# Order of users of two PSUM banks, stacked taps, a copy by DMA and a gate on other engines in a four-layer convolution and attention kernel

## The chip, the cores and the metric

The kernel runs on one core of one Trainium2 chip. The metric is the device time of one execution in microseconds. All times are of that core; a profile is one execution recorded by the hardware profiler.

## What is computed

The input x has 4 samples of 256 channels on a 48 x 48 grid (2304 positions), float32 throughout. Four layers follow, each added to x after a group norm of x over 32 groups:

```
x = x + attention(gn(x))     # layer 0: 8 heads of 64; q and k normed over positions
x = x + gated(gn(x))         # layer 1: gate from pooled, blurred, depthwise-filtered x
x = x + nonlocal(gn(x))      # layer 2: one head of 64; output normed over the batch
x = x + refine(gn(x))        # layer 3: channel gate, depthwise 3x3, instance norm, leaky

# layer 0, per sample
q, k, v = split(w_qkv @ x)
q, k = l2norm(q), l2norm(k)                  # along the 2304 positions
out = w_out @ (softmax(10 * q.T @ k) @ v) + b_out

# layer 1
t = blur_pool(max_pool_3x3(x), stride=3)     # 16 x 16
s = conv_h1(t) + conv_v1(t) + skewed_h2(t) + skewed_v2(t)   # depthwise 11x3 and 3x11
gate = sigmoid(bn(s));  out = x * upsample(gate)

# layer 2
theta, phi, g = theta_w @ x, phi_w @ x, g_w @ x              # 64 channels each
y = softmax(theta.T @ phi / 8) @ g.T;  out = batchnorm(W_w @ y)

# layer 3
a = sigmoid(w2 @ leaky(w1 @ mean(x)));  y = depthwise_3x3(x * a) + b
out = leaky((y - mean(y)) / sqrt(var(y) + eps))
```

The four depthwise filters of layer 1 add up to one filter of 81 distinct taps per channel.

## The kernel before

**Units and groups.** Attention works on units: 384 queries of one pair of heads (layer 0: 4 samples x 4 pairs x 6 = 96 units) or of one sample (layer 2: 4 x 3 = 12 units, two halves of the queries in the two halves of the partitions). A unit has 18 key blocks of 128, taken two at a time: nine groups a unit. A group issues its scores (`scores`, L322, quarter-array products of 64x64, and the exponential L328 on ScalarE), and after that the weighted sums of the group before (`weigh`, L342). Row sums are taken by adding the exponentials up on VectorE (`add_up`, L362 and L368), with halves on GpSimd for some groups (L353). There are eight buffers of exponentials, two for a group.

**Tables by group.** `attend` walks over the groups. Everything else is hung on a group: `fills` and `due` map a group's number to jobs; a job of `fills` has a rank, and the jobs of one group run in the order of their ranks, between the scores and the weighted sums. The order of issue on every engine is the order of the program. In layer 0, group 2 of each unit (`AT_CHUNK`) carries a chunk of the next pair's projection: q (rank 1), v (2), the square sum of q (2.2), k (4.5), its eviction, square sum and the next load (4.7). It also carries the output projection of the unit before (`out_proj`; first half at 2.5, or 0 in sample 0; second at 4), the row sums of that unit (`total`, 4.6), a group norm's column products (`of_means`, `of_squares`, 4.65, read at 4.8) and, in a pair's last chunk, the bias of the values two pairs on (`norms`, after all of them). After some ranks (`EVICTED`) one of layer 1's products on ScalarE (`take_taps`) is let in.

**Banks.** All these products go through two PSUM buffers, `pj`, each one bank, handed out in turn. A tile's users, on whatever engine, keep the order of the program. `of_k` lets the row sums and the norm's products use spare columns of k's bank. So one chunk uses: q first bank, v second, output 0 first, output 1 second, k first, with sums and norm columns behind k. In sample 0 the first output comes ahead of q.

**Row sums.** `total` multiplies the sums into rows, ScalarE copies them (`row`, L386), SP's queue sends them to a partition-wise layout (L388), `invert` takes the reciprocal on VectorE two groups later (L392), SP's queue sends it back and spreads it (L396, L401), and `divide` (L419) multiplies it in on GpSimd nine groups after the unit's end.

**Layer 1.** The first three samples run under layer 0: pooling on VectorE (`maxima`), products of taps on ScalarE (L899), sums on VectorE (L922). The last sample runs under layer 2 as four lanes (`l1_last`), generators that take one step a group, except in a unit's first group: the norm, `tops` (pooling of both channel halves), `sums` and `gates` (gate, statistics, and the norm for layer 2). `sums` runs `strips_pe` for one channel half after the other: 81 taps in seven rounds of twelve, each tap a diagonal 64x64 matrix (`build`, L950, on GpSimd) times a window of the padded map `pd` (L966), four quarter-array products abreast, in two banks; ScalarE copies four quarter results (L974) and VectorE adds them (L981, L984). Groups in `taken` carry other work for `pj`, and no round is issued there.

**Layer 2's projection.** `project2` computes for each slice of 384 positions phi and theta in one product (`both`, L1081) and g in another (`g`, L1102). ScalarE copies phi into both halves of the keys `kd` (L1087), and theta into `qv` (L1092). Sample 0's slices lie in the last pair's chunks of layer 0, those of samples 1 and 2 two at a time in layer 2's groups, those of sample 3 in `follow`, which waits for the norm, takes three steps, and lays out what is left in the last group of sample 2.

**Layer 3.** Tiles of one sample and channel half go through the conv (L1753) in six steps of 24 products. Each step's events run by rank. `put_before` brings the next tile: product (L1530), addition onto x (`grow`, L1592), squares; pads are shifted into four row groups by DMA and by engines (L1630 to L1636). A `Chain` for each sample turns square sums into the channel gate, in steps placed by `GATE_AT`; its matrix products write into spare columns of the conv's bank (`g_tile`) and VectorE reads them there (L1683, L1701).

Of the kernel before, what the change touches and what calls it, by code (L numbers as in the profile page):

```python
# [17 lines left out]
NK = 2  # L18
# [60 lines left out]
def usual_path(  # L79
# [40 lines left out]
    nc.gpsimd.memset(mhalf, -0.5)  # L120
    vec = cpool.tile([P, 9, NK], F32, name="vec")
# [65 lines left out]
    of_k, clock = {}, {"t": -1}  # L187
# [12 lines left out]
    def gn(b, res, halves=range(NK), slices=range(NSL), first=False, placed=False):  # L200
# [62 lines left out]
        if placed:  # L263

            t = clock["t"] + 1
            t += (AT_AFTER - t) % NG
            fills.setdefault(t, []).extend([(4.65, of_means), (4.8, squares)])
            fills.setdefault(t + NG, []).extend([(4.65, of_squares), (4.8, inverse)])
            due.setdefault(t + NG + 3, []).append(done)
            yield 1  # L270
            return
# [100 lines left out]
    def total(u):  # L372

        if of_k.get("t") == clock["t"]:
            ps = of_k["ps"][:, 392 : 392 + QC]
        else:
            ps = pj_tile()[:, :QC]
# [78 lines left out]
    EVICTED = (1, 2, 4, 4.7)  # L456
# [3 lines left out]
    def last(u, t):  # L460
# [12 lines left out]
        else:  # L473
            at_total = AT_TOTAL if "shift" in u["of"] else AT_CHUNK
            todo = [
                (fills, at_total, (4.6, lambda: total(u))), (due, AT_FOLD, lambda: fold(u, nc.gpsimd)),
# [79 lines left out]
    def project(b, norm, pair):  # L556
# [17 lines left out]

        def norms():

            w = at["w"]
            ps = pj_tile()
            for k in range(NK):
                nc.tensor.matmul(  # L580
                    ps[:, 0:1], lhsT=w[:, k, 2, :], rhs=norm["nb"][:, k : k + 1],
                    start=k == 0, stop=k == NK - 1,
                )
            pair["bias_v"] = small.tile([P, 1], F32, tag="bias_v", name="bias_v", bufs=3)
            nc.vector.tensor_copy(pair["bias_v"], ps[:, 0:1])
# [72 lines left out]
        def chunk(s):  # L658
# [7 lines left out]
            def end():  # L666
                at["evict"]()
                square(s, 1)
                if s + 2 < NCH:
                    fetch(s + 2)  # L670

            return [
                (1, query), (2, lambda: values(s)), (2.2, lambda: square(s, 0)), (4.5, key),
                (4.7, end),
# [10 lines left out]
        def rescale(c0, c1):  # L685
# [10 lines left out]
            "prefetch": prefetch, "norms": norms, "start": start,  # L696
# [6 lines left out]
    def out_proj(b, p, c, pair, o):  # L703

        cols = slice(c * SL, (c + 1) * SL)

        def part(k):
            ps = pj_tile()
# [4 lines left out]
            )  # L713
            if c == 0:
# [12 lines left out]
        return [((2.5 if b else 0, 4)[k], lambda k=k: part(k)) for k in range(NK)]  # L727
# [23 lines left out]

    def tap_weights():
# [6 lines left out]
        nc.gpsimd.tensor_add(ident2, ident[:, 0:D], ident[:, D:P])  # L759
        yield 2  # L760
# [21 lines left out]
        while i < len(TAPS):  # L782
# [6 lines left out]
            yield 1  # L789
        v1 = lp.tile([P, NK], F32, name="v1")  # L790
# [6 lines left out]
    WEIGHT_TICKS = 26  # L797

    NT = 4
# [3 lines left out]
    L1_BUF = (NT + 1) * AS * AS  # L803
# [123 lines left out]
    TAPS_AT_ONCE = 12  # L927

    AT_PLACE = 7

    def strips_pe(b, k, norm, res):


        rounds = [
            range(i, min(i + TAPS_AT_ONCE, len(TAPS)))
            for i in range(0, len(TAPS), TAPS_AT_ONCE)
        ]
        diag = {}
        acc = lp.tile([P, AS, AS], F32, tag=("l1acc", "blur2")[k], name="l1acc")
        res["acc"] = acc  # L940
        parts = wo.rearrange("p c n -> p (c n)").rearrange(
            "p (i h r c) -> p i h r c", i=2, h=2, c=AS
        )

        def build(n):
            taps = rounds[n]
            xs = xsp.tile([P, NK, SL + 1], F32, tag="xs", name="diag1")
            xs = xs.rearrange("p k s -> p (k s)")[:, : len(taps) * D]
            diag[n] = xs.rearrange("p (t j) -> p t j", j=D)
            nc.gpsimd.tensor_tensor(  # L950
                diag[n], ident2.unsqueeze(1).to_broadcast([P, len(taps), D]),
                wt[:, k, taps[0] : taps[-1] + 1].unsqueeze(2).to_broadcast([P, len(taps), D]),
                ALU.mult,
            )

        def product(n):
            taps = rounds[n]
            ps = [pj_tile()[:, : AS * AS] for _ in HALVES]
            runs = [taps[0::2], taps[1::2]]
            for i in range(len(runs[0])):  # L960
                for h, r in enumerate(HALVES):
                    for e, run in enumerate(runs):
                        if i >= len(run):
                            continue
                        dr, dc = TAPS[run[i]]
                        nc.tensor.matmul(  # L966
                            ps[h][HALVES[h ^ e]].rearrange("p (r c) -> p r c", c=AS),
                            lhsT=diag[n][r, run[i] - taps[0], :],
                            rhs=pd[r, PAD + dr : PAD + dr + AS, PAD + dc : PAD + dc + AS],
                            start=i == 0, stop=i == len(run) - 1,  # L970
                        )
            for h, r in enumerate(HALVES):
                for e in range(2):
                    nc.scalar.copy(  # L974
                        parts[r, n % 2, e].rearrange("p r c -> p (r c)"), ps[h][HALVES[h ^ e]]
                    )

        def add(n):
            two = parts[:, n % 2]
            if n == 0:  # L980
                nc.vector.tensor_add(acc, two[:, 0], two[:, 1])  # L981
                return
            for e in range(2):
                nc.vector.tensor_add(acc, acc, two[:, e])  # L984
# [3 lines left out]
        while "blurred" not in res or "nb" not in norm:  # L988
            yield 1
        pd = padded(k, norm, res)  # L990
# [1909 lines left out]
```

## Time and profile before

| | us |
|---|---|
| median of 3 runs | 3505.92 |
| lowest, highest | 3504.39, 3508.83 |
| profiled execution, its own time | 3503.65 |
| its span | 3501.90 |
| PE busy | 3430.2 (98%) |
| VectorE busy | 2541.1 (73%) |
| ScalarE busy | 2331.2 (67%) |
| GpSimd busy | 793.9 (23%) |

How to read it: "busy" is the time in which an engine had an instruction at work; matmuls are pipelined, their ends are modelled, and a wait shorter than the pipeline is not seen in "busy", only in the distance between starts. Layer 0 runs from the start to about 2896 us, layer 2 (with layer 1 of the last sample) to about 3341, layer 3 to the end. The profile's lines that carry the argument stand in the prediction.

### The profile page before, as it was taken

How to read it: one execution, taken by the hardware profiler on the slowest of the kernel's cores; microseconds unless marked ns; L12 is line 12 of the kernel's file. 1: busy time of each engine (PE TensorE's matmuls, PEld its weight loads, DVE VectorE, ACT ScalarE, POOL GpSimd, SP SyncE). 2: the span in 40 equal slices, each digit the busy share in tenths (PEclk: the TensorE clock that was granted, in tenths of full speed). 3: DMA queues.
4: the chain of work that ended last, by engine and by line, in shares of the span. 5: the costliest groups of instructions: out<-in, count | busy, mean ns of one | idle time of the engine just before them, and what ended most of it. 6: DMA issues, size and time to landing. Idle time of an engine off the chain costs nothing.

```text
span 3501.9 us, 89386 instructions
## 1 busy us (share of the span) xinstructions
PE 3430.2 (98%) x37990; PEld 1728.2 (49%) x37990; DVE 2541.1 (73%) x3352; ACT 2331.2 (67%) x3751; POOL 793.9 (23%) x668
## 2 busy tenths in 40 slices
PE   9999999999999999999999999999999999999988
PEld 5454545454444444444444444444444444554533
DVE  3455545467788788687887886868887879757677
ACT  5555655555885686557866875568658855555577
POOL 2333333320101010001110100001010106667432
PEclk9999999999999999999999999999999999999999
DMA  2211111111111111121111111111111110000057
GB/s 90 49 27 22 26 22 22 27 22 27 22 32 22 26 22 26 43 58 22 27 17 26 22 26 22 27 12 32 16 30 13 31 13 6 6 6 8 4 144 234
DMA packets 102759, 116.33 MB, mean 33 GB/s; under 512 B 39712, under 2 KB 93840, under 8 KB 101584
## 3 DMA queue, kind: packets, MB, share of 16 engines
q1 hardware_dynamic: 101104, 108.63, 16.4%
q8 instruction: 300, 4.92, 0.6%
q10 hardware_dynamic: 1248, 1.91, 0.2%
q14 instruction: 107, 0.88, 0.1%
HBM read 56.99 MB, written 11.80 MB: 20 GB/s over the span
## 4 chain that ended last, share of the span: by engine, by line
PE 86%; DVE 9%; issue 2%; ACT 1%; POOL 1%; DMA 1%; DVEq 0%; SPq 0%; POOLq 0%; ACTq 0%
PE av L342 33%; PE sc L322 33%; PE pj L615 8%; PE pj L710 3%; PE pj L649 3%; DVE acc L368 3%; PE cv L1753 2%; PE pj L381 1%; PE pj L966 1%; PE pj L1081 1%; DVE x L1029 1%; ACT kd L1087 0%; DVE x L1848 0%; DVE x L723 0%; DMA sh<-pad 0%
## 5 line engine op out<-in xcount | busy, mean ns | idle before, releaser
L328 ACT ACTIVATE pt<-sc 128x768 f32<-128x768 f32 x1944 | 1473.4, 810 | 696.8 <-PE sc L322 692.6
L368 DVE TENSOR_TENSOR acc<-acc,pt 128x768 f32<-128x768 f32 x1368 | 1362.8, 996 | 209.6 <-ACT pt L328 114.3
L342 PE MATMUL av<-pt,v 64*64 64x384 f32 x13824 | 1274.7, 484 | 0.0
L322 PE MATMUL sc<-q,k 64*64 64x384 f32 x13824 | 1269.9, 482 | 0.5 <-ACT pt L328 0.5
L322 PEld LDWEIGHTS sc<-q,k 64*64 64x64 f32 x13824 | 525.5, 133 | 589.4 <-issue 558.5
L342 PEld LDWEIGHTS av<-pt,v 64*64 64x64 f32 x13824 | 518.2, 133 | 564.4 <-issue 521.6
L419 POOL TENSOR_TENSOR o<-o,rinv 128x384 f32<-128x384 f32 x95 | 117.4, 1236 | 1702.5 <-DMA rinv<-rinv 1691.4
L353 POOL TENSOR_TENSOR half<-pt 128x768 f32<-128x768 f32 x189 | 365.8, 1939 | 508.9 <-ACT pt L328 438.5
L368 DVE TENSOR_TENSOR acc<-acc,half 128x768 f32<-128x768 f32 x171 | 187.1, 1094 | 223.3 <-POOL half L353 222.5
L899 ACT ACTIVATE prod<-pd,wt 128x256 f32<-128x256 f32 x486 | 340.7, 761 | 0.2
L723 DVE SCALAR_TENSOR_TENSOR x<-pj,bo,x 128x384 f32<-128x384 f32 x192 | 118.1, 617 | 256.0 <-PE pj L710 254.7
L615 PE MATMUL pj<-xs,w 128*128 128x384 f32 (+1 forms) x720 | 277.5, 508 | 3.9 <-DVE x L723 3.9
L615 PEld LDWEIGHTS pj<-xs,w 128*128 128x128 f32 x720 | 124.0, 189 | 143.6 <-DVE x L723 28.8
L342 PE MATMUL av<-pt,qv 64*64 64x384 f32 x1728 | 171.9, 494 | 0.0
L322 PE MATMUL sc<-qv,kd 64*64 64x384 f32 x1728 | 167.9, 485 | 2.4 <-ACT pt L328 2.4
L922 DVE TENSOR_REDUCE prod<-prod 128x256 f32<-128x1280 f32 x114 | 168.7, 1480 | 0.3 <-ACT prod L899 0.3
L710 PE MATMUL pj<-o,wo 128*128 128x384 f32 (+1 forms) x384 | 159.7, 513 | 5.2 <-issue 3.6
L649 PEld LDWEIGHTS pj<-w,xs 128*128 128x128 f32 x1080 | 134.5, 191 | 24.1 <-issue 1.2
L386 ACT COPY row<-pj 128x96 f32<-128x96 f32 x104 | 24.9, 240 | 179.3 <-PE pj L381 179.3
L362 DVE TENSOR_TENSOR acc<-pt 128x768 f32<-128x768 f32 x99 | 113.5, 1146 | 41.9 <-ACT pt L328 41.9
L415 POOL TENSOR_TENSOR o<-raw 128x384 f32<-128x384 f32 x95 | 120.5, 1269 | 72.7 <-ACT raw L411 72.6
L649 PE MATMUL pj<-w,xs 128*128 128x128 f32 x1080 | 134.9, 275 | 0.0
(292 smaller groups left out, 2364.3 us busy)
## 6 DMA issues: line engine op xcount, KB each, us to landing
xs<-in_x_dram SPq DMA_DIRECT2D x90, 384.0 KB
sh<-pad SPq DMA_DIRECT2D x126, 162.2 KB
rinv<-rinv SPq DMA_DIRECT2D x208, 94.5 KB
out_dram<-x SPq DMA_DIRECT2D x23, 384.0 KB
w<-in_wqkv_dram SPq DMA_DIRECT2D x32, 192.0 KB
x<-in_x_dram SPq DMA_DIRECT2D x4, 1152.0 KB
x<-in_x_dram SPq DMA_DIRECT2D x9, 384.0 KB
rinv<-ls SPq DMA_DIRECT2D x208, 1.5 KB
```

The costliest lines, as they stand in the source:

```text
L322: nc.tensor.matmul(ps[c * D : (c + 1) * D, h, :SL], lhsT=u["of"]["k"][r, j0 : j0 + D], rhs=u["of"]["q"][r, u["qc"]], start=True, stop=True,)
L328: nc.scalar.activation(pt, ps[:, :, :SL], AF.Exp, scale=u["scale"])
L342: nc.tensor.matmul(u["av"][h * D : (h + 1) * D, half, :SL], lhsT=value(u, j, h)[r], rhs=pt[r, h, :], start=j == 0, stop=j == JB - 1,)
L353: nc.gpsimd.tensor_add(half, pts[0], pts[1])
L368: nc.vector.tensor_add(u["acc"], u["acc"], term)
L415: eng.tensor_add(u["sum"], u["raw"][:, 0, :], u["raw"][:, 1, :])
L615: nc.tensor.matmul(ps[:, :n], lhsT=at["w"][:, k, t, :], rhs=xs[s][:, k, :n], start=k == 0, stop=k == NK - 1,)
L649: nc.tensor.matmul(ps[:, i * P : (i + 1) * P], lhsT=xs[s][:, k, i * P : (i + 1) * P], rhs=at["w"][:, k, 2, :], start=k == 0, stop=k == NK - 1,
L710: nc.tensor.matmul(ps[:, :n], lhsT=wo[:, p, k * P : (k + 1) * P], rhs=o["o"][:, :n], start=True, stop=True,)
L723: nc.vector.scalar_tensor_tensor(xs, ps[:, :SL], pair["bo"][:, k : k + 1], xs, ALU.add, ALU.add)
L899: nc.scalar.activation(bufs[n % 3][:, :, min(n, 1) + i].rearrange("p (r c) -> p r c", c=AS), pd[:, PAD + dr : PAD + dr + AS, PAD + dc : PA ...
L922: nc.vector.tensor_reduce(to, bufs[n % 3][:, :, : min(n, 1) + len(taps)], AX.X, ALU.add)
```

## The change

It has five parts. Cut to its core, in the order of the file:

1. **Ranks in layer 0.** k comes at 3 (was 4.5), its eviction at 3.2, its square sum and the load at 4.3. The second output product stays at 4; its addition onto x is split off (`onto`) and comes at 4.2. The row sums come at 4.1 and use spare columns of the second output's bank (`of_out`) instead of k's. The norm's column products come at 3.1, read at 3.3, still in k's bank; the values' bias product is split off (`biased`) and comes at 3.05 in k's bank.

```diff
-            fills.setdefault(t, []).extend([(4.65, of_means), (4.8, squares)])
-            fills.setdefault(t + NG, []).extend([(4.65, of_squares), (4.8, inverse)])
+            fills.setdefault(t, []).extend([(3.1, of_means), (3.3, squares)])
+            fills.setdefault(t + NG, []).extend([(3.1, of_squares), (3.3, inverse)])
...
-        if of_k.get("t") == clock["t"]:
-            ps = of_k["ps"][:, 392 : 392 + QC]
+        if of_out.get("t") == clock["t"]:
+            ps = of_out["ps"][:, 392 : 392 + QC]
...
-    EVICTED = (1, 2, 4, 4.7)
+    EVICTED = (1, 2, 3.2, 4.3)
...
-                (1, query), (2, lambda: values(s)), (2.2, lambda: square(s, 0)), (4.5, key),
-                (4.7, end),
+                (1, query), (2, lambda: values(s)), (2.2, lambda: square(s, 0)), (3, key),
+                (3.2, lambda: at["evict"]()), (4.3, end),
...
-        return [((2.5 if b else 0, 4)[k], lambda k=k: part(k)) for k in range(NK)]
+        return [
+            (2.5 if b else 0, first), (4, lambda: part(1)), (4.2, lambda: onto(1)),
+        ]
```

2. **Stacked taps.** Under layer 0 the tap weights are also laid out four deep (`stacked`: copies on GpSimd, 16 DMAs on SP's queue). In layer 2, `strips_pe` handles both channel halves. For 32 channels at a time, four shifted copies of their padded map are stacked in the four row groups by DMA, so that one product of 128 rows and 32 columns adds four taps; 21 stacks take the place of 81 taps. There are eight fillings (`ORDER3`) of 16 DMAs each, in three sets of buffers, at most eight DMAs a step; a round follows three steps or more after the filling's last DMA. Ten rounds of three or six stacks take one bank each.

```diff
+        def place(u, n):
+            k, i, _ = ORDER3[u]
+            start, step, size, _ = STACKS[i]
...
+            nc.sync.dma_start(
+                bufs[u][j // 2][32 * q : 32 * q + 32, c0 : c0 + size],
+                pd[k][32 * j : 32 * j + 32, start + step * q : start + step * q + size],
             )
...
+            ps = pj_tile()[:, : AS * AS]
+            for m in range(m0, m1):
+                for j in range(4):
+                    c0 = (j % 2) * size + offsets[m - FIRST3[i]]
+                    rhs = bufs[u][j // 2][:, c0 : c0 + AS * PW]
+                    nc.tensor.matmul(
+                        ps[32 * j : 32 * j + 32].rearrange("p (r c) -> p r c", c=AS),
+                        lhsT=diag[n][:, m - m0, j, :],
+                        rhs=rhs.rearrange("p (r c) -> p r c", c=PW)[:, :, 0:AS],
+                        start=m == m0, stop=m == m1 - 1,
                     )
...
+            if u in placed and seen >= placed[u] + SETTLED and clock["t"] not in taken:
+                product(n)
+                n += 1
+                if n + 1 < len(rounds):
+                    build(n + 1)
+            for _ in range(FILLS_AT_ONCE):
+                if not left or not may_fill(left[0][0], n):
+                    break
+                v, c = left.pop(0)
+                place(v, c)
```

3. **Phi by DMA.** ScalarE evicts phi once; a DMA on SP's queue copies it into the other half of the keys. For sample 0, g comes at rank 2.7 (was 2), after the first output product.

```diff
-            for r in HALVES:
-                nc.scalar.activation(
-                    s2["k"][r, s * SL : (s + 1) * SL], ps[phi], AF.Identity,
-                    bias=at["bias"][phi, 0:1],
-                )
+            nc.scalar.activation(
+                s2["k"][phi, cols], ps[phi], AF.Identity, bias=at["bias"][phi, 0:1]
+            )
...
+            nc.sync.dma_start(s2["k"][theta, cols], s2["k"][phi, cols])
```

4. **Layer 3's gate.** ScalarE reads the chain's columns out of the bank; sums, reciprocals (as a power) and products go to GpSimd; the leaky step stays on VectorE. The steps are placed anew, and the check of the row sums (`judge`) is read by ScalarE too.

```diff
-                nc.vector.tensor_copy(raw, of["ps"])
+                nc.scalar.copy(of["raw"], of["ps"])
...
-                nc.vector.tensor_scalar(ga, ga, 1.0, None, ALU.add)
-                nc.vector.reciprocal(ga, ga)
+                pool.tensor_scalar(ga, ga, 1.0, None, ALU.add)
+                pool.tensor_tensor(ga, ga, mone, ALU.pow)
...
-        0: (3, 5, 6, 7, 9, 10, 11, 12, 13), B - 1: (-2, -1, 0, 1, 3, 4, 5, 6, 7),
+        0: (3, 5, 6, 9, 10, 11, 11, 12), B - 1: (-2, -1, 0, 3, 4, 5, 7, 8),
...
-        GATE_AT[n] = (-2, 1, 2, 3, 5, 6, 9, 10, 11)
+        GATE_AT[n] = (-2, 1, 2, 5, 6, 7, 9, 10)
```

5. **Constants.** A column of -1 (`mone`), and more steps for the lane of the tap weights (`WEIGHT_TICKS`, 26 to 34).

## The prediction

> **What bounds the kernel now.** The first page gives TensorE (PE) busy 98% of the span. So only two things can shorten it: fewer or shorter products, or fewer of the gaps between them. I cut the span into stages with the view of busy time by windows (columns: stretch and its length; busy us and instructions of PE, weight loads, VectorE (DVE), ScalarE (ACT), GpSimd (POOL); clock, DMA share, GB/s).
>
> ```profile
> 800.00:2720.00 1920.00, 1911.05 (x21128) 943.12 (x21124) 1529.65 (x1987) 1381.95 (x2238) 197.60 (x172) 1.00 0.16 26
> 2896.00:3245.00 349.00, 325.83 (x3785) 187.19 (x3778) 253.48 (x295) 187.62 (x309) 233.40 (x125) 0.98 0.07 6
> 3341.00:3502.00 161.00, 138.49 (x1462) 54.23 (x1462) 120.78 (x229) 126.08 (x196) 49.15 (x111) 0.95 0.75 205
> ```
>
> Layer 0 idles PE 9 us in 1920; layer 2 up to its last sample 23 in 349; layer 3 22 in 161. "Busy" hides short waits, so I read starts in the timeline of PE. One steady slot of layer 0 with a projection in it:
>
> ```profile
> 2010.34 1.56 PE L615 MATMUL pj<-xs,w 128*128 128x385 f32 x4
> 2011.74 1.50 PE L649 MATMUL pj<-w,xs 128*128 128x128 f32 x12
> 2013.07 1.65 PE L710 MATMUL pj<-o,wo 128*128 128x384 f32 x4
> 2014.60 1.56 PE L615 MATMUL pj<-xs,w 128*128 128x385 f32 x4
> 2016.09 0.54 PE L381 MATMUL pj<-acc,step 128*32 128x96 f32 x16
> 2016.56 1.20 PE L342 MATMUL av<-pt,v 64*64 64x384 f32 x12
> ```
>
> From start to start: q 1.40, v 1.33, both output products 1.53, k 1.49, sums 0.47; 6.22 us. All through layer 0 a group of sixteen quarter-array products of 384 columns, four abreast, starts 1.29 us after the one before, so one pass of 384 columns is 0.3225. The four of the outputs need 1.29; they take 1.53, 0.24 of it waiting. The weight loads split it: the first output lasts 0.73 (0.645 and a wait of 0.09 for the eviction of v), the second 0.79 (0.645 and 0.145 until VectorE has read the first output, for k takes its bank). Where a norm's column product follows the sums, it adds 0.3 for itself and holds PE idle before:
>
> ```profile
> 1596.75 0.54 PE L381 MATMUL pj<-acc,step 128*32 128x96 f32 x16
> 1597.64 0.38 PE L245 MATMUL pj<-gn_sq,gmat 128*128 128x2 f32 x2 [0.36 <-ACT row L386]
> 1597.96 1.52 PE L342 MATMUL av<-pt,v 64*64 64x384 f32 x16
> ```
>
> Sums to product 0.89 instead of 0.47, plus 0.32: 0.74 us. Layer 2's double projection and a round of layer 1's taps:
>
> ```profile
> 2922.17 2.85 PE L1081 MATMUL pj<-x,w 128*128 128x384 f32 x8
> 2925.57 1.55 PE L1102 MATMUL pj<-w,x 128*128 128x64 f32 x12 [0.55 <-ACT qv L1092]
> 2927.34 1.55 PE L1102 MATMUL pj<-w,x 128*128 128x64 f32 x12 [0.23 <-ACT qv L1092]
> 2928.83 1.52 PE L342 MATMUL av<-pt,qv 64*64 64x384 f32 x16
> 2972.78 2.92 PE L966 MATMUL pj<-pd,diag 64*64 64x256 f32 x48 [1.76 <-ACT pd L882]
> 2975.49 1.50 PE L342 MATMUL av<-pt,qv 64*64 64x384 f32 x16
> ```
>
> g waits for ScalarE, which copies phi twice and theta once for each slice. In layer 3 PE is stopped by VectorE, itself stopped while it wants to read a column of a bank that ScalarE is evicting:
>
> ```profile
> 3410.98 0.88 PE L1530 MATMUL w<-y,Ww 64*64 64x384 f32 x8 [3.29 <-DVE hraw L1701]
> 3468.88 0.60 PE L1708 MATMUL cv<-hl,w 64*128 64x1 f32 x4 [2.77 <-DVE hl L1703]
> ```
>
> **The Trainium skill.** "PSUM — Partial Sum Buffer", Terms, says that two engines may not touch one bank and quadrant at once, reads included. The trace agrees in effect: VectorE's read of the norm's columns (L236) waits 21.2 us in 8 times for ScalarE's read of k in the same bank. So every bank has one order of users, and the change is a change of that order. "TensorEngine Tiling (Array Packing)", Key Properties, says that a change of tiling mode drains the array. Here the run before a switch is 0.11 longer (64x64 to full) or 0.20 (full to 32 columns), and sums take 0.47 where 16 products of 96 columns, four abreast, need 0.32. "DMA: Bandwidth & Descriptors", Issuing engines are not separate DMA queues, says all issuers share 16 engines; layer 3 shows a share near 1, layer 2 only 0.07.
>
> **Layer 0.** New order of banks: q A, v B, output 0 A, k B (norm columns behind it, in B), output 1 A, sums in A. k now waits for v's eviction exactly as output 1 did (0.09). Output 1 waits for VectorE's read of output 0, but k's 1.29 lie between. Gone: the rest of the gap, 0.145 in each of 64 slots of samples 1 to 3 (9.3), and what late VectorE reads or evictions add over the smallest slot (6.1 summed over those 64; mostly VectorE, so I take all). Sample 0 (output first, 6.06 a slot): the wait for v moves behind k, 0.085 x 23 = 2.0. Norm products: 17 slots; directly behind k they cost 0.24 (what two such cost at the start, where nothing switches) instead of 0.74: 8.5. The v bias product moves too (0.54 to about 0.44) x 14 = 1.4. Sum 27.3.
> The price: VectorE's read of output 1 now stands behind ScalarE's copy of the sums. Output 1 was read at 4.4 us into the slot; now at about 6.1 + 0.3 + 0.24 + 0.1 = 6.8, so VectorE is some 2.4 later, and the adds of exponentials queue behind. Cover: VectorE idles 0.93 before output 0, then 1.29 of k; it has 1529.65 of 1920 busy, about 6 us free a slot period. After the slot its debt can grow to some 2.4, while eight buffers of exponentials hold four groups of 2.58. I take 0. If the whole debt reached the next slot, each would stall 2.4 - 0.93 - 1.29 = 0.2: 12 us.
> Last pair (layer 2's first projection in 6 slots, 5.70 each): output 0 now lies between both and g, g starts after two evictions instead of three: 5.5, gain 1.2.
>
> **Layer 2, taps.** A pass of 256 columns is 0.215. Now 648 products, four abreast: 34.8, with 0.1 at each of 14 rounds 36. New: 21 stacks x 4 quarters x 2 passes x 2 channel halves = 336, four abreast: 18.1, and ten switches to 32 columns and back at 0.3: 21. Gain 15. The 56 copies (20.5 us of ACT) become ten of 256 columns, 26 adds become eight.
> 128 DMAs of 60 to 81 KB come onto SP's queue, 0.59 us each as layer 3's pad copies: 16 take 9.4 us. They go past the row sums' and reciprocals' DMAs. A product comes three steps after the last issue, groups of about 3.2 us, so data are there; a sum's DMA waits behind at most eight, 4.7 us, where two groups (6.5) lie before VectorE's reciprocal. I take 0, ends 0 and +15. POOL's pad clearing for the second half waits for pad reads, about 3 us once.
> **Phi by DMA.** ACT does two evictions of 0.58 a slice, not three. After the first slice g waits 0.3 + 1.16 - 1.29 = 0.17 where it waited 0.7; the second not at all: 1.2 x 6 = 7.2. The 24 DMAs land slices before keys are read.
> **The end of the lanes.** Counting the generators' steps by groups of layer 2: rounds now fall in groups 20 to 56, gates begin at 38 and 58, the norm is done at 77, theta's weights start at 79, all six slices come at the last group, 80, as the trace has them (2972.8, 3151.9, 3227.0, 3230.6). New: products at 24, 29, 33, 42, 46, 47, 51, 53, 55, 60; gates at 47 and 61; norm, start and slices all at 80. PE then waits for the norm's last two VectorE operations behind an add and POOL's half sum: +2.5. The six slices (19.8 now, a 0.63 wait in five, 0.13 left) save 2.5. Net 0.
> **Stalls in layer 2.** I find 22 us of gaps before taps, statistics and their successors (the largest 4.25 before L1135 at 3190.8). VectorE and ScalarE lose 13 and 31 us of work and a round needs one bank, not two; but the second gate comes 3 groups later, beside the statistics. I take -5, ends -15 and +8. Layer 2: -27.2.
>
> **Layer 3.** Reads go to ScalarE in its own order, VectorE no longer stands: 3.3, 1.7 and 2.8 of PE waits go. But the DMA share is 1 in the middle, so some is lost to pad copies; POOL's power and products make the last scale a step later, waited for by VectorE at the end. I take -4, ends -9 and +4.
> Extra weight staging (some 30 small POOL copies of 0.24, 16 DMAs) lies under layer 0, where POOL is a third busy: 0.
>
> **Sum.** 27.3 + 1.2 + 27.2 + 4 = 60 off. Against its own 3503.65 us (span 3501.90 and 1.75 around it): 3444. The median shown is 2.27 above: 3446.
>
> **Rivals.** (A) As above, 0.62; own range 3430 to 3462. (B) Layer 2 gives back: late fills, the second gate on the statistics, the exposed norm: layer 2 nets 5, layer 3 nothing; 3505.9 - 33.5 = 3472, 0.20. For: that stage already loses 22 us to VectorE's order. Against: work is taken off both busy engines. (C) VectorE's relief clears nearly all gaps (10 more) and layer 3's 8 go whole: 3432, 0.09. (D) No change, 3506, 0.03: VectorE's debt carried on in 64 slots at 0.94 each; against it the 0.93 + 1.29 cover. (E) Slower: SP. If each of eight batches held SP for 20 us (waiting for a buffer or pd while the sums' DMA stands behind), VectorE would stand at the reciprocal, in order, and PE beyond the 10.3 us that four groups cover: 8 x 10 = 80, so 3446 + 80 = 3526. It decides above 17.5 us a batch; issue alone is 9.4. 0.06.
> Range 3428 to 3480: A, C and most of B. What a measurement of this kernel tells from no change is about 0.2% (7 us). A, B and C are faster by more: 0.91; within: 0.03; slower: 0.06.
>
> **What would show it.** Slots in layer 0 of about 6.06 us from q to the next product, no wait of k's or output 1's loads for VectorE, norm products right behind k; taps in ten runs of 1.6 to 2.9; g waits under 0.2; no 3 us gaps in layer 3. It is wrong if VectorE's read of output 1 shows up as PE waits, if the reciprocal L392 waits for its DMA, or if PE waits for pad stacks.

## The result and the profile after

| | before | after |
|---|---|---|
| median, us | 3505.15 (4 runs) | 3461.71 (4 runs) |
| lowest, highest | 3503.98, 3508.83 | 3459.98, 3462.47 |
| ratio, 95% interval | | 0.9874 (0.9857 to 0.9891) |
| span of the profiled execution | 3501.9 | 3459.7 |

The change takes 43 us off; 60 were forecast. Four marks cut both spans into five stretches. They are starts of TensorE instructions: the first scores, the first bias product ahead of theta for sample 0 (from there the last pair of layer 0 carries layer 2's projection), the same for sample 1 (layer 2), and the first weighted sums after sample 3's six slices (from there on, layer 2's last sample and layer 3).

| stretch | before | after | difference | forecast |
|---|---|---|---|---|
| start, to the first scores | 39.8 | 44.0 | +4.2 | 0 |
| layer 0 without its last pair | 2684.3 | 2657.2 | -27.1 | -27.3 |
| last pair | 186.7 | 188.4 | +1.7 | -1.2 |
| layer 2, samples 0 to 2, and the slices of sample 3 | 339.6 | 318.2 | -21.4 | -27.2 |
| last sample of layer 2, layer 3 | 251.5 | 251.9 | +0.4 | -4 |

The sum is -42.2, the difference of the spans. The three stages that the prediction shows for the kernel before, here for the changed kernel, by windows (columns as there: PE, weight loads, VectorE, ScalarE, GpSimd, clock, DMA share, GB/s):

```profile
800.00:2697.00 1897.00, 1896.63 (x21108) 945.08 (x21104) 1536.10 (x1986) 1378.44 (x2237) 195.82 (x172) 1.00 0.15 26
2874.00:3203.00 329.00, 308.32 (x3453) 163.29 (x3445) 240.53 (x276) 161.02 (x247) 226.30 (x121) 0.98 0.19 37
3298.00:3460.00 162.00, 138.60 (x1462) 56.85 (x1462) 116.19 (x193) 126.21 (x205) 70.26 (x151) 0.96 0.73 204
```

In layer 0 PE idles 0.4 us instead of 9. In layer 2 the stretch is 20 us shorter, but PE still idles 21 us of it, where it was 23: the products went, the gaps stayed. In layer 3 PE idles 23 of 162 us, one more than before. A slot of layer 0 after, in the timeline of PE (start, duration, engine, line, operation), and one with a norm's product:

```profile
1994.51 1.56 PE L625 MATMUL pj<-xs,w 128*128 128x385 f32 x4
1995.91 1.50 PE L659 MATMUL pj<-w,xs 128*128 128x128 f32 x12
1997.25 0.81 PE L723 MATMUL pj<-o,wo 128*128 128x384 f32 x2
1997.98 1.56 PE L625 MATMUL pj<-xs,w 128*128 128x385 f32 x4
1999.38 0.81 PE L723 MATMUL pj<-o,wo 128*128 128x384 f32 x2
2000.12 0.54 PE L383 MATMUL pj<-acc,step 128*32 128x96 f32 x16
2000.58 1.52 PE L344 MATMUL av<-pt,v 64*64 64x384 f32 x16
...
1584.68 0.28 PE L247 MATMUL pj<-gn_sq,gmat 128*128 128x2 f32 x2
1584.82 0.89 PE L723 MATMUL pj<-o,wo 128*128 128x384 f32 x2
```

From q to the weighted sums it takes 6.07 us instead of 6.22: each output product takes 0.73 or 0.74, and no wait is shown. The norm's product takes 0.14 behind k, and the output after it 0.82 instead of 0.73. Layer 2's projection, and a round of stacked taps:

```profile
2900.91 2.85 PE L1199 MATMUL pj<-x,w 128*128 128x384 f32 x8
2903.74 2.89 PE L1220 MATMUL pj<-w,x 128*128 128x64 f32 x24
2906.56 1.52 PE L344 MATMUL av<-pt,qv 64*64 64x384 f32 x16
...
2966.93 3.19 PE L1061 MATMUL pj<-y,diag 128*32 128x256 f32 x48 [1.68 <-DVE bst L1263]
2970.05 1.20 PE L344 MATMUL av<-pt,qv 64*64 64x384 f32 x12
```

The projection takes 5.65 us for two slices instead of 6.66, without a wait for ScalarE. The round takes 3.12 us from start to start; the mean of the four long ones is 2.96, of the six short ones 1.52: 4 x 2.96 + 6 x 1.52 = 21. But a wait of 1.68 stands ahead of this one.

**The start.** The values of the first pair, in the timeline of PE; before first:

```profile
31.34 8.20 PE L649 MATMUL pj<-w,x 128*128 128x128 f32 x72
...
39.81 1.52 PE L322 MATMUL sc<-q,k 64*64 64x384 f32 x16
```

and after:

```profile
31.33 1.50 PE L659 MATMUL pj<-w,x 128*128 128x128 f32 x12
33.40 1.60 PE L659 MATMUL pj<-w,x 128*128 128x128 f32 x12 [0.57 <-ACT v L664]
...
43.97 1.52 PE L324 MATMUL sc<-q,k 64*64 64x384 f32 x16
```

The six blocks ran as one before. Now each after the first waits for ScalarE's eviction of the block before, as if there were one bank only.

**Layer 2.** What PE waited for from the first mark of sample 1 to the end of the slices (columns: total us, times, longest), before:

```profile
PE pj L966 <- DVE bst L1143: 5.1, 3, 2.4
PE pj L1102 <- ACT qv L1092: 4.7, 12, 0.6
PE pj L1135 <- DVE bst L1143: 4.5, 2, 4.3
PE pj L1081 <- ACT qv L1092: 2.8, 5, 0.6
```

and after:

```profile
PE pj L1255 <- DVE bst L1263: 6.2, 3, 3.5
PE pj L1061 <- DVE bst L1263: 4.0, 2, 2.3
PE pj L233 <- DVE bst L1263: 2.7, 1, 2.7
```

The 7.5 us of waits for ScalarE are gone. The waits for VectorE's `bn_stats` went from 9.6 to 12.9; these are the statistics for layer 2's batch norm, and until VectorE has read a product for them, the product holds its bank of `pj`. The third row is new. It is this place in the timeline of PE:

```profile
3170.31 0.82 PE L1255 MATMUL pj<-y,Ww 64*64 64x384 f32 x8
3173.87 0.59 PE L233 MATMUL pj<-mx,gmat 128*128 128x2 f32 x2 [2.74 <-DVE bst L1263]
3174.39 2.84 PE L344 MATMUL av<-pt,qv 64*64 64x384 f32 x16
3177.01 2.78 PE L324 MATMUL sc<-qv,kd 64*64 64x384 f32 x16
```

The norm's means product of sample 3 finds both banks held by the statistics of sample 2. Before, the lanes were three groups ahead and the two did not meet. And the stop costs twice: the sums and scores after it start 2.6 us apart instead of 1.29. The windows of that place say why (the clock is the third last column):

```profile
3174.40:3177.00 2.60, 2.60 (x17) 1.02 (x20) 1.89 (x8) 0.00 (x0) 0.60 (x1) 0.50 0.00 0
3177.00:3179.60 2.60, 2.60 (x24) 1.00 (x20) 0.00 (x0) 0.81 (x1) 0.00 (x0) 0.50 0.03 1
```

The clock granted is 0.50. Against a run without waits the place loses 2.92 us to the wait and 0.20 + 1.33 + 1.27 + 0.43 after it, about 6.2 in all (the means product takes 0.52 where it took 0.32 before).

That a stop costs twice is not new with the change. The largest stop of layer 2 before, ahead of the last statistics of sample 1, has the same after it (a line of PE's timeline and a window, both of the kernel before):

```profile
3190.81 2.01 PE L1135 MATMUL pj<-y,Ww 64*64 64x384 f32 x8 [4.25 <-DVE bst L1143]
3190.80:3194.70 3.90, 3.89 (x24) 2.55 (x28) 3.90 (x8) 0.00 (x0) 2.91 (x2) 0.50 0.00 0
```

This stop stayed: 3.5 us in the changed kernel, the longest wait of the first row.

**Layer 3.** The waits for VectorE's chain that the prediction shows (3.29 and 2.77 us) are gone. Two others stand in the changed kernel that the kernel before has not (PE's waits, columns as above):

```profile
PE cv L1802 <- POOL gn_sq L1798: 2.9, 1, 2.9
PE w L1650 <- DVE sound L2042: 1.9, 1, 1.9
```

The first is for GpSimd's sums of the gate, the second stands behind the check of the row sums, which now comes later on VectorE.

### The profile page after: what moved, and what is told of

The parts are those of the page before. It is cut to its first block, busy times and chain, and to the rows that moved or that the text cites. A ratio compares the mean times of both kernels' runs of the same rounds, so it can differ in the third digit from the quotient of the medians.

```text
span 3459.7 us, 88715 instructions
## 1 busy us (share of the span) xinstructions
PE 3397.6 (98%) x37678; PEld 1711.7 (49%) x37678; DVE 2540.6 (73%) x3298; ACT 2297.1 (66%) x3690; POOL 824.9 (24%) x734
## 3 DMA queue, kind: packets, MB, share of 16 engines
q1 hardware_dynamic: 109936, 119.53, 17.1%
## 5 line engine op out<-in xcount | busy, mean ns | idle before, releaser
L413 ACT COPY raw<-av 128x768 f32<-128x768 f32 x108 | 86.4, 800 | 48.3 <-PE av L344 47.8
## 6 DMA issues: line engine op xcount, KB each, us to landing
rinv<-rinv SPq DMA_DIRECT2D x208, 94.5 KB
```

## The experiments

All medians are of four runs or more, and each ratio is to runs of the kernel before on the same chip (its median 3506.2 to 3508.4 there). The stretches of every profile:

| kernel | median | start | layer 0 | last pair | layer 2 | rest |
|---|---|---|---|---|---|---|
| before | 3505.15 | 39.8 | 2684.3 | 186.7 | 339.6 | 251.5 |
| after | 3461.71 | 44.0 | 2657.2 | 188.4 | 318.2 | 251.9 |
| p_order | 3489.80 | 44.2 | 2658.2 | 189.0 | 344.4 | 254.0 |
| p_stack | 3490.52 | 39.7 | 2684.5 | 186.7 | 326.6 | 250.7 |
| p_phi | 3498.16 | 39.8 | 2684.2 | 186.2 | 330.4 | 254.1 |
| p_gate | 3506.40 | 39.8 | 2684.2 | 186.7 | 341.7 | 251.8 |
| e_fix | 3455.82 | 40.1 | 2657.4 | 188.7 | 317.1 | 250.3 |
| e_stats | 3461.01 | 44.1 | 2658.0 | 188.4 | 319.3 | 249.9 |
| e_lane | 3465.60 | 43.9 | 2657.3 | 186.8 | 323.3 | 252.1 |
| e_last | 3461.82 | 44.0 | 2657.7 | 188.4 | 318.6 | 255.5 |
| e_fixact | 3450.87 | 39.9 | 2657.3 | 187.2 | 316.7 | 252.5 |
| e_split | 3447.85 | 39.8 | 2657.5 | 188.4 | 309.9 | 250.9 |
| e_lane2 | 3454.70 | 39.8 | 2657.7 | 186.9 | 314.8 | 250.1 |

How far one profile can be read: p_gate changes nothing in layer 2, and its layer 2 differs from before's by 2.1 us (clock by windows 0.97 instead of 0.98). The clock records give the size: in layer 2 PE is busy at a clock of 0.50 for 12.9 us before and for 16.6 in p_gate. What is done at half clock takes twice as long, so half of the difference, 1.8 us, is an estimate of what the clock took. Such estimates follow where they change a reading.

By their ratios the four parts alone save 0.53, 0.50, 0.25 and 0.01%, together 1.29%; the whole saves 1.26%. So the parts hardly stand in each other's way, and what is missing against the forecast is missing in the parts too.

### Parts alone

Each is the kernel before with one part of the change.

p_order: part 1.

> Kernel before with the order of layer 0 alone (q, v, output, k, output; norm and bias products in k's bank, sums in the output's). Theory: the first group's scores still start about 4.1 us late, because the bias product of pair (0, 1) in the prologue takes columns of the prologue's last k tile and holds its bank; layer 0 then loses 27 us and the last pair 1.2: 3505.1 + 4.1 - 27.3 - 1.2 = 3481. Rival: the late start comes from another part (staging, the new constant tile on GpSimd), so the scores start at 39.8 us as before and the time is 3477. Layer 2's products and stalls as before, within 2 us, by both.

3489.80 us, ratio 0.9947 (0.9930 to 0.9963). The first scores come at 44.2: the late start belongs to this part. Layer 0 is 26 us shorter. But 8 us of the expected 24 are missing: the last pair, layer 2 and the rest grew by 2.3, 4.8 and 2.5, where theory and rival had a gain of 1.2 in the last pair and nothing after it. Layer 2's waits for `bn_stats` do not explain it (5.1 and 4.5, as before). The clock does in size: PE is busy at a clock of 0.50 for 3.4, 20.0 and 12.8 us of these three stretches, and before for 0, 12.9 and 6.8. Half of the difference, an estimate, is 1.7 + 3.6 + 3.0, some 8 us. It is not this one profile alone: the mean granted clock is 0.994, 0.994, 0.995 and 0.994 in the four runs, and 0.995 or 0.996 in 19 of the 21 runs of the kernel before beside them. Why this order lets the clock fall more often was not tried.

p_stack: part 2.

> Kernel before with the stacked taps alone. Theory: the ten products take 21 us instead of 36, but the lanes end three groups later, so that the norm's means product of sample 3 falls into the groups in which w_stats of sample 2 holds the projection banks: stalls grow by about 8, and the time is 3505.1 - 15 + 8 = 3498. Rival: the growth of the stalls comes from phi's copy by DMA, so the 15 us come whole, or with the forecast's 5 more: 3485 to 3490. Prologue and layer 0 as before by both.

3490.52 us, 0.9950 (0.9934 to 0.9967). The rounds take 21 us instead of 36, and layer 2 is 13 shorter. The time is the rival's (3485 to 3490), not the theory's 3498. The collision is there all the same, without phi's DMA (timeline of PE):

```profile
3200.68 0.59 PE L231 MATMUL pj<-mx,gmat 128*128 128x2 f32 x2 [2.76 <-DVE bst L1239]
```

So the theory is right on where the collision comes from, the taps, and wrong on what it costs in all: other gaps shrank, and of 15 us 2 were given back, not 8.

p_phi: part 3.

> Kernel before with phi's second copy by DMA alone. Theory: both and g take 1.1 us less in each of six slices and nothing else moves: 3505.1 - 6.5 = 3498.6. Rival: the DMA, which is queued on SyncE behind the layer's other loads, lets the scores of the next sample or the lanes wait, and half or more is given back: 3502 to 3505.

3498.16 us, 0.9975 (0.9965 to 0.9984). The projections of layer 2 are 9.3 us shorter: 1.0 in each of five pairs of slices, 1.4 in the sixth, and 2.9 in the last six slices (19.77 to 16.90), which the expectation left out. No wait for the DMA shows. The stretch itself is 9.2 shorter and the rest 2.6 longer in this profile; PE's time at half clock is 6.1 us less in the one and 5.8 more in the other, so about 3 us of each is the clock, and some 3 us of what the projections saved went to longer waits (those for `bn_stats` are 10.5 us instead of 9.6, those for ScalarE's padded map 2.8 instead of 1.8).

p_gate: part 4.

> Kernel before with layer 3's gate on ScalarE and GpSimd alone. Theory: the old waits for VectorE's chain go (-7 to -8), GpSimd's sums, the first conv's transfers and the tail's later gate bring as much back: 3505.1, within 2 us, with the last stretch (after the last products) about 2 us longer. Rival: the forecast's -4 holds, and what was lost in layer 3 beside it came from the other parts (an earlier end of layer 2 leaves less time for staging): 3501.

3506.40 us, 0.9999 (0.9990 to 1.0008). The profile shows both halves of the theory. After the last conv come 24 products without a use of their own, which keep TensorE running (L198 before, L200 here). From the slices' end to these it takes 229.6 us instead of 232.5, and from these to the end 22.2 instead of 19.1. Lines of PE's timeline for p_gate:

```profile
3455.64 0.38 PE L1684 MATMUL cv<-gn_sq,gmat 128*128 128x2 f32 x2 [2.02 <-POOL gn_sq L1680]
3482.05 2.94 PE L200 MATMUL w<-gmat 128*128 128x128 f32 x24
3488.95 2.70 PE L1880 MATMUL w<-x,ident 128*128 128x384 f32 x4 [2.66 <-DVE x L1860]
```

and the last place in the kernel before:

```profile
3487.66 1.56 PE L1868 MATMUL w<-x,ident 128*128 128x384 f32 x4 [0.57 <-DVE x L1848]
```

PE waits for GpSimd's sums where it waited for VectorE, and at the end 2.66 us for VectorE's last step, which waits for the later scales; before, that wait was 0.57. The old waits of 3.29 and 2.77 us were each followed by 3.4 us at a clock of 0.50, and so is the new one at the end: with them moved a part of what they cost.

### The changed kernel with one thing altered

e_fix, the start:

```diff
-            if of_k.get("t") == clock["t"]:
+            if clock["t"] >= 0 and of_k.get("t") == clock["t"]:
                 at["ps"] = of_k["ps"][:, 504:505]
```

> The changed kernel, with the bias product of pair (0, 1) kept out of the prologue's last k tile (it takes a tile of its own before the first group). Theory: the values' six blocks start 1.34 us apart again instead of 2.17 us, the first group's scores come at 39.8 us instead of 44.0, and the whole span shifts by as much: 3461.7 - 4.1 = 3457.6. Rival: the late values have another cause (the evictions on ScalarE), or the loads behind the first phase set its start, and the time stays at 3461.7.

3455.82 us, 0.9852 (0.9836 to 0.9869); scores at 40.1. PE's timeline:

```profile
31.60 8.20 PE L659 MATMUL pj<-w,x 128*128 128x128 f32 x72
...
40.08 1.52 PE L324 MATMUL sc<-q,k 64*64 64x384 f32 x16
```

The theory of the late start is shown: one comparison brings the scores back. Both time stamps in the prologue are -1, so `biased` took a column of the last k tile, and that bank stayed taken until then. The median fell by 6 us, where 4.1 were expected; the mean granted clock is 0.996 or 0.997 in these runs.

e_stats, the collision moved away:

```diff
-            spread(work, stats(b, 0), [22, 23])
+            spread(work, stats(b, 0), [23, 25] if b == 2 else [22, 23])
```

> The changed kernel, with w_stats of sample 2's first chunk in groups 77 and 79 instead of 76 and 77, so that the norm's two products of sample 3 (groups 76 and 78) meet none of them. Theory: of the 6.3 us of stalls in groups 76 to 78 (2.92 + 0.32 + 1.33 + 1.27 + 0.43) at least 4 go, and the next sample's theta, phi and g, which wait for the norm, start no later: 3461.7 - 4 = 3457.7. Rival: the stalls are VectorE's bn_stats as such and move along with w_stats, or the norm then comes later and its wait before theta takes the place: 3461, within 2.

3461.01 us, 0.9866 (0.9850 to 0.9883): no gain. The 6 us are gone from their place; what came instead (PE's timeline):

```profile
3181.45 0.38 PE L247 MATMUL pj<-gn_sq,gmat 128*128 128x2 f32 x2 [1.55 <-DVE bst L1263]
...
3189.14 0.58 PE L1163 MATMUL pj<-gn_nb,w2c 128*128 128x1 f32 x4 [1.34 <-DVE gn_nb L262]
...
3191.80 2.66 PE L1220 MATMUL pj<-w,x 128*128 128x64 f32 x12
```

The rival holds: the wait moved to the norm, with its stretch of half clock behind it (this g takes 2.45 us to the next start instead of 1.43; the slices take 20.7 instead of 17.8).

e_lane, the lanes earlier:

```diff
-    FILLS_AT_ONCE = 8
-    SETTLED = 3
+    FILLS_AT_ONCE = 16
+    SETTLED = 2
```

> The changed kernel, with 16 instead of 8 loads of a stack issued per group and the products let go two instead of three groups after the last load. By the lanes' rules the products then come at groups 24, 26, 29, 38, 42, 46, 47, 51, 53, 55 instead of 24 to 60, and the norm's means product at 70, before w_stats. Theory (lateness of the lanes makes the collision): the stalls of 6.3 us at groups 76 to 78 and the 1.2 us before theta go, so 3461.7 - 6 = 3455.7, less what a product loses where its loads have not landed. Rival: a product in these earlier groups meets bn_stats or late loads (each load takes some 0.6 us of SyncE's queue, 16 of them more than a group), and the time is 3461 to 3466.

3465.60 us, 0.9880 (0.9864 to 0.9897), the rival's value. Loads are late, and theta waits for `bn_stats` all the same (PE's timeline):

```profile
2993.69 3.27 PE L1061 MATMUL pj<-y,diag 128*32 128x256 f32 x24 [1.45 <-DMA y<-pd]
...
3182.73 1.01 PE L1163 MATMUL pj<-gn_nb,w2c 128*128 128x1 f32 x4 [2.90 <-DVE bst L1263]
```

e_last, the last sample's gate as before:

```diff
+            if self.n == B - 1:
+                steps = [
+                    (MID, total_dve), (SMALL, groups), (MOMENTS, inverse_dve),
+                    (MID, pooled_dve), (SMALL, first_layer), (MOMENTS, hidden_dve),
+                    (SMALL, second_layer), (FRONT, gate), (FRONT, scaled_dve),
+                ]
...
-        ..., B - 1: (-2, -1, 0, 3, 4, 5, 7, 8),
+        ..., B - 1: (-2, -1, 0, 1, 3, 4, 5, 6, 7),
```

> The changed kernel, with the gate of the last sample in layer 3 as in the kernel before (its sums, scales and gate on VectorE, the gate ready one step earlier). Theory: the stretch from the last products of layer 3 to the end takes 16.2 us again instead of 18.2, and the wait of the last groups product for GpSimd's sums (2.88 us) goes as well, while the wait before second_layer (2.98 us before) comes back: 3461.7 - 2 = 3459.7. Rival: the tail is set by ScalarE's and VectorE's own queue and stays at 18.2 us; with the wait for VectorE back the time is 3464.

3461.82 us, 0.9868 (0.9851 to 0.9884), between theory and rival. From the keep-warm products to the end 18.3 us instead of 21.0; ahead of them 237.2 instead of 230.9 in the profiled run, which has a lower clock (0.995) than two of the other three (0.997). One wait in PE's timeline is the old one, and longer:

```profile
3430.64 1.01 PE L1836 MATMUL cv<-hl,w 64*128 64x1 f32 x4 [3.98 <-DVE hl L1831]
```

What the end gained was lost ahead of it, where waits for VectorE are back. How much of that is VectorE's chain is not shown: PE is busy at half clock for 13.0 us of the rest in this profile and for 6.8 in the changed kernel's, an estimated 3 us of the 6. By the medians this gate costs the same on either engine.

### Is VectorE what layer 2 waits for?

By windows, VectorE is busy for 59.70 of the first 62 us of layer 2 before and for 59.95 after: the cut products relieve it of nothing there. e_fixact (on e_fix) takes the bank out of its hands: ScalarE copies the product, and VectorE reads the copy.

```diff
+            y = op.tile([P, SL + 1], F32, tag="o", name="wy")[:, :SL]
+            nc.scalar.copy(y, ps)
-            nc.vector.bn_stats(bst[:, k, b * NSL + s, :], ps)
+            nc.vector.bn_stats(bst[:, k, b * NSL + s, :], y)
```

> e_fix, with the products of w_stats copied from their bank by ScalarE (two copies of 384 columns a group) and bn_stats read from the copy, so that a bank comes free without VectorE. Theory: the stalls of layer 2 are VectorE's queue (in the changed kernel busy for 59.95 of the first 62 us of layer 2 after the last pair) seen through the banks that bn_stats holds; at 3146, 3170, and ahead of the products at 2963, 3004 and 3078 they add up to some 15 us, of which at least 8 go: 3455.8 - 8 = 3448 or less. Rival 1: VectorE's work is conserved and its lateness shows at the next instruction that waits for it (sums, l1acc, norm), less than 2 us go: 3454 to 3456. Rival 2: the copies stand behind the exponentials on ScalarE and hold the banks as long: 3456 or more.

3450.87 us (3448.64 to 3455.44), 0.9837 (0.9824 to 0.9851), about 5 us below e_fix's 3455.82 (3452.96 to 3457.97); the ranges overlap, and it lies between theory and rival 1. PE's waits in layer 2, where e_fix has 11.5 us for `bn_stats`:

```profile
PE sc L324 <- ACT pt L330: 5.1, 3, 2.2
PE pj L1163 <- DVE gn_nb L262: 4.8, 1, 4.8
PE pj L233 <- DVE mx L222: 2.9, 1, 2.9
```

(This profile is of the slowest of the five runs.) No wait for `bn_stats` is left, and 7.7 us of waits for VectorE stand at the norm of sample 3, the first thing in which PE cannot do without it; in e_fix 1.2 us did. So rival 1 holds for more than half. A part of rival 2 shows too: the scores' wait for ScalarE's exponentials went from 2.2 to 5.1 us. Then e_split (on e_fixact) takes work off VectorE: in samples 0 to 2 the last half of a chunk is no longer added up; the product of the row sums takes it beside the accumulator.

```diff
+            if u.get("split"):
+                u["rest"] = ready.pop()
...
+        of = [u["acc"]] + ([u["rest"]] if "rest" in u else [])
+        for i, e in [(i, e) for i in range(len(of)) for e in range(2)]:
```

> e_fixact, with the last of a chunk's nine halves in layer 2 (samples 0 to 2) no longer added by VectorE: the product of the sums takes it beside the accumulator, 16 more tiny products a chunk. VectorE is relieved of 9 additions of 1.1 to 1.5 us, some 12 us, and TensorE pays 9 x 0.33 = 3 us. Theory (the work on VectorE's path to the next sample's norm is what layer 2 waits for): the waits ahead of theta, phi and g (5.0 + 4.3 us in e_fixact) and of the norm (3.1) go for the most part: 3450.9 + 3 - 9 = 3445. Rival: VectorE's path waits for GpSimd's halves anyway, and one of three half buffers is now held longer, so GpSimd and behind it the exponentials wait: 3451 to 3458.

3447.85 us (3446.18 to 3449.71), 0.9825 (0.9809 to 0.9842). The median lies between theory (3445) and rival (3451 and more), 3 us below e_fixact; ranges and intervals of the two overlap. VectorE's busy time up to theta went from 233.9 to 222.7 us, as intended. But the waits that the theory wanted gone are nearly as long as before, two of PE's waits in layer 2:

```profile
PE pj L1167 <- DVE gn_nb L262: 4.6, 1, 4.6
PE pj L1259 <- DVE gn_gm L238: 2.4, 1, 2.4
```

Layer 2 takes 309.9 us in the profile, 6.8 less than in e_fixact's. PE is busy at half clock for 5.0 us of it and for 17.1 in e_fixact's, so an estimated 6 of the 6.8 are the clock. Whether the relief of VectorE raised the clock, by fewer or better placed waits, or whether the two profiles met the clock differently by chance, is not shown. So the theory, that work on VectorE's path is what layer 2 waits for, fits and is not proved. What is shown is both steps together: e_split's runs are all faster than e_fix's (3452.96 to 3457.97). It is the fastest version run, 14 us under the changed kernel.

e_lane2 is e_fixact with e_lane's two numbers.

> e_fixact, with 16 loads of a stack per group and two groups from the last load to the first product, as in e_lane. Theory: the banks no longer wait for VectorE, so of e_lane's new stalls only those within a product, which wait for loads, stay (2.03 + 1.92 + 2.08 = 6 us), and the norm of sample 3 comes six groups earlier and gives VectorE the slack to end before theta (5.0 + 4.3 us go): 3450.9 + 6 - 9 = 3448. Rival: VectorE's lateness is independent of the groups in which the lanes' steps are issued, since its queue is full; the waits before theta stay and the loads' come on top: 3455 to 3458.

3454.70 us, 0.9846 (0.9830 to 0.9863), next to the rival's value, though for another reason. The wait of theta's bias products is 1.0 instead of 4.8, as the theory has it, but the loads take as much (PE's waits in layer 2):

```profile
PE pj L1061 <- DMA y<-pd: 5.2, 2, 3.8
PE pj L383 <- DVE acc L370: 3.1, 1, 3.1
```

## Why the prediction was right, and where it was off

The forecast (A) held in direction, and 3461.7 lies just inside the upper edge of its own range (3462) and inside the range given. It is nearer to B's 3472 than to A's 3446: of 60 us 43 came. Point by point:

- **Layer 0: right, in its parts less exactly than in its sum.** "Sum 27.3"; 27.1 in the profile. The slots of samples 1 to 3 gave 21.3 of the 23 that their terms add up to, and the rest of layer 0 gave 5.8 instead of 4; that the two cancel is luck. The mechanism is as told: plain slots take 6.06 at the median instead of 6.21, those with a norm's column product 6.29 instead of 6.95. Its "debt" of VectorE at 0 held: the read of the second output waits for ScalarE's copy of the sums as foreseen (94.5 us over the samples 1 to 3), but VectorE's waits for exponentials fell from 121.4 to 62.0, and PE's waits for VectorE's read of an output fell from 3.9 us in 16 times to 0.3 in one.
- **The start: missed.** The prediction had no term for it. It read `biased` as a move inside a slot and did not follow the call that runs before any slot exists. +4.2, shown by e_fix.
- **Last pair: -1.2 foreseen, +1.7 came.** Five slots went from a mean of 5.70 only to 5.57, as g waits 0.62 for theta's eviction. Where the norm's second product stands between the outputs, the place takes 3.58 instead of 3.02, and the half clock that follows costs 1.8 us (0.64 on the mean from 2883.3 to 2888.0). p_order has the like, +2.3.
- **"Phi by DMA ... 7.2" and "The six slices save 2.5": right.** The projections are 9.3 us shorter alone (p_phi), 6.5 and 2.9.
- **"Taps ... Gain 15": right in size** (36 to 21); so was "Net 0" for the lanes' end, with 1.0 us of wait ahead of theta and 2.9 saved in the slices. The fillings were hidden: no wait in the changed kernel names a stack's load. One of 1.8 us ahead of a round names nothing; it is gone in e_fixact, which leaves the loads as they are, so a bank is the likelier cause. e_lane shows how near the limit the loads are.
- **"Stalls in layer 2 ... I take -5": the step that failed**, with "VectorE and ScalarE lose 13 and 31 us of work" as its reason. Taps and phi gave their 25, the stretch only 21.4: the stalls and the norm's wait grew by about 3.5 where -2.5 was forecast. The lanes end three groups later, and the norm's product meets the statistics (p_stack). The work taken off lies mostly where VectorE had room (36.5 of 65 us busy at 3045 to 3110 before, 27.6 of 60 at 3020 to 3080 after). Moving the collision (e_stats) moves the wait, freeing the banks (e_fixact) moves more than half of it. That VectorE is what the stage waits for is made likely by these waits, which name it wherever they turn up; e_split, which takes work off it, does not settle it.
- **"Layer 3 ... I take -4": two waits missing, the end mis-sized.** The waits of 3.3 and 2.8 us went, as foreseen. The third, of 1.7, was no wait: behind the wait of 3.29 the next 24 products of the conv take 3.77 us from start to start instead of 2.07, at a clock of 0.50. In their place came 2.9 us for GpSimd's sums and 1.9 behind the check of the row sums, and the prediction had a term for neither. Alone, the way to the end takes 2.9 us less and the end 3.1 more (p_gate); in the whole it is 1.6 less and 2.0 more. "Waited for by VectorE at the end" was named and not priced.

Of the rivals, B had the place (layer 2 gives back) but not the size: layer 2 netted 21, not 5. C, D and E are excluded by the measured time; no instruction waited ahead of the reciprocal (L394 here), as E needs. E's limit of 17.5 us a batch should read 17.8 (10.3 and an eighth of 60), which changes nothing.

The sum of what was missed is 4.2 at the start, 2.9 in the last pair, 5.8 in layer 2, 4.4 after it and 0.2 in layer 0: 17.5, the difference between 59.7 (the parts of the forecast as the table has them) and 42.2.

What stays open: why p_order's clock is lower, and what e_split's 3 us come from.

## What to carry to other kernels

Where a job finds its place by a time stamp, follow it also to the calls before the clock runs: two equal "not yet" stamps tied up a bank and cost 4 us. When products are cut from a stage in which another engine is full, ask for the dependency at which its lateness will show next: moving the meeting point moved the wait. And before a few us between two profiles are put down to a change, compare the time that each spent at half clock. Taking reads off one engine is a gain only if the step does not come later where nothing follows that could hide it.

## What was not expected of the hardware

- **A short wait can cost twice.** After the wait of 2.74 us PE ran at a granted clock of 0.50 for more than 5 us and lost 3 us more; in the last pair waits of 1.16 and 0.28 were enough. The Trainium skill, "TensorE: Matmul & The Clock Gate", section "HAM oscillation — how this bites in real kernels", gives as the rule to have no gap over about 3.4 us. Here shorter ones were enough, and the measurement decides. Other waits of the kind (2.30 ahead of 3008.3 and 1.85 ahead of 3082.0 in the changed kernel) were followed by no such stretch.
- **Where a wait falls decides what it costs.** In all thirteen traces the granted clock changes between 1.00 and 0.50 only at the points of a grid of 3.413 us, and where the grid lies against the kernel's start differs from trace to trace. From 2820 us on, cut along this grid, every window at full clock in which PE, with work still to come, idled 2.0 us or more was followed by one at half clock, 49 of 49; of those with 1.3 to 2.0 us idle 17 of 90, of those with less 6 of 377. The wait of 2.74 has 2.5 us in one window; the one of 2.30 is divided by a point of the grid into 0.4 and 1.9. So a wait of 2 to 3 us can cost nothing more or 3 us more, by chance of the execution. The same page, "What's actually happening", has a free-running window of 3413 ns, about one period of this grid, and the traces agree. These counts are a regularity of thirteen traces; no run was made to test it.
- **The mean granted clock differs between versions** of the same work, 0.994 to 0.997 by run. 0.001 of the span is 3.5 us, as much as most of the terms argued over here.
- **An add costs more beside GpSimd.** VectorE's addition of exponentials takes 1.00 us in the last pair, where GpSimd is busy 23 of 189 us, and 1.13 to 1.47 in the stretches of layer 2, where it is busy some 70%. The operands differ (exponentials in one, GpSimd's halves in the other), but they are not the cause: over the changed kernel's trace the 1240 adds of either kind that run beside no GpSimd instruction take 0.96 us at most, and those that overlap one for half their time or more take 1.28 (76 adds of exponentials) and 1.46 (35 of halves) on the mean, 2.6 at most. The skill's "SBUF — State Buffer", "Who interferes with whom", has a VectorE instruction with two inputs in SBUF contend with a GpSimd instruction that reads SBUF; the trace agrees in effect. The prediction counted instructions on VectorE and left that out.
